# Newton roots on VectorE, a router in four column parts, a hand-ordered token choice and tile-wise memory waits in a two-layer transformer kernel

## The chip, the cores and the metric

The kernel runs on one core of one Trainium2 chip. The metric is the device time of one execution in microseconds (us); lower is better. The engines are PE (TensorE: matmuls and transposes; PEld are its weight loads), DVE (VectorE), ACT (ScalarE), POOL (GpSimd) and SP (SyncE, which here issues most DMAs). Each engine works through its own queue in order.

## The reference

Two layers on x of 2 x 2048 tokens of width 512, with a context of 154 rows per batch, all in float32:

```python
x = x + L0_xattn(layernorm(x), ctx)     # 16 heads of 32, softmax
x = x + L0_ffn(layernorm(x))            # 8 experts; each takes its 1024 best tokens
x = x + L1_xattn(layernorm(x), ctx)     # one head of 512
x = x + L1_ffn(layernorm(x))            # shared part, and 2 of 8 experts per token

def L0_ffn(x):
    scores = softmax(x @ router_w + router_b)
    G, idx = top_k(scores.T, 1024)
    h1 = relu(x[idx] @ w1 + b1)
    eo = h1 @ w2 + b2
    return zeros.at[idx].add(eo * G)

def layernorm(x):
    return (x - mean) / sqrt(var + 1e-5)
```

## The kernel before

The 4096 tokens are 32 tiles of 128 rows (`NT`), in 8 blocks of 4 tiles (`NB`, `TPB`). Five stages follow one another.

**Attention of the first layer.** Inside `tc.manual_schedule` the order on PE, DVE, ACT and POOL is the order in which the program is written. `step(G)` runs for G = 0 to 37; with m, i4 = divmod(G, 4) it handles four heads (i4) of block m, in four quarters. A quarter makes the scores of one token tile (`scores_of`: eight matmuls into the single PSUM tile `sc`, L285, then the row maximum `mx` on DVE, L289, and a subtraction, L290), takes exp on ACT (`exp_of`, L301 and L304) and normalizes the quarter before (`normalize`: sum and reciprocal on DVE, L310 and L311, a product on POOL, L312). Between these stand the transposes `pp` of the previous step's probabilities (L318), the products with the values `av` (L333), the queries of the next block (L186), and behind the attention the output projection (L352), the residual (L357), and the norm and router of older tiles: `norm_x1`, `transpose_x1`, `router`, `logits`, `router_scores`. `router(u)` is called for one tile and multiplies `rw` of 512 x 8; `logits` turns the four results of a block with four small transposes.

`roots(m)` makes the reciprocal standard deviations of one block of x and one of the residual stream: Sqrt on ACT (L161), then a reciprocal on DVE (L162). It is called in the steps with i4 = 2; its readers are `norm_x` and `norm_x1` (L166). After 38 steps a written tail finishes the last block.

**Token choice.** The pools of the attention close. The pool `wm` (weights of the experts, two tags `w1` and `w2` of four buffers of 1 MB) and then `sr` and `pr` open in their memory. Here the order is not written by hand; the framework's scheduler makes it. SP loads the second layer's context weights, then four `w1` and four `w2` tiles. `scores` is turned (L573) and copied to `sco` (L574). A search fixes the 30 bits of each expert's threshold: a count on DVE (L591), a matmul that adds it up per expert (`per_expert`, L579), two small operations on DVE (L594, L595). Then positions are counted, down to `hi` and `lo` (L633, L634). Beside it PE projects the second layer's context (`ps_k`, `ps_kw`, `ps_bqk`, `ps_v`, L643 to L668), whose results go to DRAM (`kw_d`, `vp_d`).

**Experts of the first layer.** The pools `se`, `sm`, `pm` open, again with an order written by hand. `list_head`, `list_part`, `list_sum` and `list_end` make expert 0's token list, `gather` fetches rows of `xs` by index (POOL), `sum_w1` (POOL, L818) and `sum_x` (DVE) prepare sums, and then 16 half-experts run as `hidden` and `outputs`, PE all the time on `product` (L710). POOL adds each result into `xacc` (L901).

**Second layer.** The pools `wh`, `wf`, `sf`, `pf`, `sf1` open. SP loads `kw`, `vp` and the weights of the shared part (L1068 to L1081), then the rows of `xacc` (L1161); steps run over the tiles, and the routed experts follow.

When a pool opens in memory that a closed pool held, its first users wait for everything that used the old pool. Within a pool, a buffer waits for the last use of that buffer alone.

Of the kernel before, what the change touches and what calls it, by code (L numbers as in the profile page):

```python
# [34 lines left out]
E = 8  # L35
# [20 lines left out]
def two_layers(ctx: ExitStack, tc: tile.TileContext, a, out):  # L56
# [36 lines left out]
    def layernorm(src, dst, small):  # L93

        st = small.tile([P, TPB, 6], F32, tag="st", name="st")
        mv = small.tile([P, TPB, 2], F32, tag="mv", name="mv")
        rstd = small.tile([P, TPB], F32, tag="rstd", name="rstd")
        for t in range(TPB):
            nc.vector.bn_stats(st[:, t, :], src[:, t, :])
            nc.vector.bn_aggr(mv[:, t, :], st[:, t, :])  # L100
        nc.scalar.activation(rstd, mv[:, :, 1], AF.Sqrt, bias=eps_t)
        nc.vector.reciprocal(rstd, rstd)
        for t in range(TPB):
            nc.vector.tensor_scalar(
                dst[:, t, :], src[:, t, :], mv[:, t, 0:1], rstd[:, t : t + 1], ALU.subtract, ALU.mult
            )
# [16 lines left out]
    with (  # L123
        tc.tile_pool(name="wa", bufs=1) as wa,
        tc.tile_pool(name="sx", bufs=2) as sx,
# [5 lines left out]
        rw = wa.tile([P, KC, E], F32, name="rw")  # L131
# [26 lines left out]
        def roots(m):  # L158
            mv, rstd = roots_of(m)
            j = slice(0 if 0 <= m - 2 < NB else 1, 2 if m + 3 < NB else 1)  # L160
            nc.scalar.activation(rstd[:, j], mv[:, j, :, 1], AF.Sqrt, bias=eps_t)  # L161
            nc.vector.reciprocal(rstd[:, j], rstd[:, j])  # L162
# [29 lines left out]
        with tc.tile_pool(name="wk", bufs=1) as wkv:  # L192
# [4 lines left out]
            for w, n in ((wk, "w_kT"), (wv, "w_vT"), (wq, "w_qT"), (wo, "w_oT"), (rw, "router_w")):  # L197
                nc.sync.dma_start(w, a[n].rearrange("(k p) n -> p k n", p=P))
# [3 lines left out]
            roots(-3)  # L202
# [12 lines left out]
            roots(-2)  # L215
# [48 lines left out]
            roots(-1)  # L264
# [6 lines left out]
        with tc.tile_pool(name="sa", bufs=2) as sa:  # L271
# [89 lines left out]
            def norm_x1(u, eng=nc.vector):  # L361
                blk, i = divmod(u, TPB)
                row[u] = sa.tile([P, ROW], F32, tag="row", name="row", bufs=8)
                norm(row[u][:, 0:D], x1t.pop(u), blk + 2, 0, i, eng)

            def transpose_x1(u):
                x1T[u] = sa.tile([P, KC, P], F32, tag="x1T", name="x1T", bufs=4)
                transpose_tile(row[u][:, 0:D], x1T[u], 0, pa, "gen", 3)

            def router(u):  # L370
                blk, i = divmod(u, TPB)
                if i == 0:
                    lT[blk] = sa.tile([E, TPB, P], F32, tag="lT", name="lT")
                ps = pa.tile([E, P], F32, tag="gen", name="ps_l", bufs=3)
                for k in range(KC):
                    nc.tensor.matmul(ps, rw[:, k, :], x1T[u][:, k, :], start=k == 0, stop=k == KC - 1)
                nc.scalar.copy(lT[blk][:, i, :], ps)
# [3 lines left out]
            def logits(blk):  # L381
                pl = pa.tile(SL, F32, tag="gen", name="pl", bufs=3)
                for t in range(TPB):
                    nc.tensor.transpose(pl[:, t, :], lT[blk][:, t, :], ident[0:E, 0:E])
                lg = sa.tile(SL, F32, tag="lg", name="lg")
                lm = sa.tile([P, TPB, 1], F32, tag="lm", name="lm")
                nc.vector.tensor_tensor(lg, pl, rb_bc.unsqueeze(1).to_broadcast(SL), ALU.add)
# [17 lines left out]
            LAST = NT - TPB  # L405

            def step(G):
                m, i4 = divmod(G, TPB)
                on, before = tile_of(G), tile_of(G - 1)
                if tile_of(G + 16):  # L410
                    load_x(G + 16)
# [6 lines left out]
                if i4 == 2 and m <= NB + 1:  # L418
                    roots(m)
# [6 lines left out]
                if tile_of(G - 11) and G - 11 < LAST:  # L426
                    transpose_x1(G - 11)
                if tile_of(G + 9):
                    norm_x(G + 9, nc.gpsimd)
                if on:  # L430
                    scores_of(G, 1)
# [9 lines left out]
                av = values(G - 2) if tile_of(G - 2) else None  # L441
                if on:
                    scores_of(G, 2)
# [11 lines left out]
                if tile_of(G - 10) and G - 10 < LAST:  # L455
                    norm_x1(G - 10, nc.gpsimd)
                if tile_of(G - 11) and G - 11 < LAST:
                    router(G - 11)
# [9 lines left out]
                if tile_of(G + 15):  # L468
                    stats(xt[G + 15], (G + 15) // TPB - 3, 1, (G + 15) % TPB)
                if i4 == 3 and tile_of(G - 15):  # L470
# [3 lines left out]
            for G in range(LAST + 10):  # L474
                step(G)
            roots(NB + 1)
            transpose_x1(LAST - 1)
            router(LAST - 1)
            for u in range(LAST, NT):
                norm_x1(u)  # L480
                transpose_x1(u)
            logits(NB - 2)
            router_scores(NB - 2)
            for u in range(LAST, NT):
                router(u)
            logits(NB - 1)
            router_scores(NB - 1)
# [4 lines left out]
    keep = ctx.enter_context(tc.tile_pool(name="keep", bufs=1))  # L492
# [4 lines left out]
    with tc.tile_pool(name="wm", bufs=4) as wm:  # L497
# [9 lines left out]

        with (
            tc.tile_pool(name="sr", bufs=1) as sr,
            tc.tile_pool(name="pr", bufs=1, space=PSUM) as pr,  # L510
        ):

            ctxT = sr.tile([P, KC, B * TKV], F32, name="ctxT")
            nc.sync.dma_start(ctxT, a["ctxT"].rearrange("(k p) n -> p k n", p=P))
            wk = sr.tile([P, KC, D], F32, name="wk1")
            wv = sr.tile([P, KC, D], F32, name="wv1")
            wqT = sr.tile([P, KC, D], F32, name="wqT1")
            for w, n in ((wk, "Wk"), (wqT, "WqT"), (wv, "Wv")):
                nc.sync.dma_start(w, a[n].rearrange("(k p) n -> p k n", p=P))
            bq = sr.tile([P, KC], F32, name="bq")  # L520
            bk = sr.tile([P, KC], F32, name="bk")
            nc.sync.dma_start(bq, a["bq"])
            nc.sync.dma_start(bk, a["bk"])
            bv_bc = sr.tile([P, D], F32, name="bv_bc")
            nc.sync.dma_start(bv_bc, a["bv"].partition_broadcast(P))
            for q in range(4):
                load_w1(0, q)
            for q in range(4):
                load_w2(0, q)

            def iota(dst, pattern, mult):
                i = sr.tile(dst.shape, I32, name="iota_i")
                nc.gpsimd.iota(i, pattern=pattern, base=0, channel_multiplier=mult)
                nc.vector.tensor_copy(dst, i)

            iota(io128, [[1, P]], 0)
            iota(io8, [[1, CAP // P]], 0)
            iota(io_t, [[1, NT]], 0)
            iota(io_p, [[1, 1]], 1)

            same = sr.tile([P, E, NR], F32, name="same")
            tri = sr.tile([P, E, NR], F32, name="tri")
            nc.gpsimd.affine_select(
                same,
                ones.rearrange("p (e r) -> p e r", e=E),
                pattern=[[-NR, E], [0, NR]],
                compare_op=ALU.is_ge,
                fill=0.0,  # L550
                base=0,
                channel_multiplier=1,
            )
            nc.gpsimd.affine_select(
                same,
                same,
                pattern=[[NR, E], [0, NR]],
                compare_op=ALU.is_ge,
                fill=0.0,
                base=NR - 1,  # L560
                channel_multiplier=-1,
            )
            nc.gpsimd.affine_select(
                tri, same, pattern=[[NR, E], [1, NR]], compare_op=ALU.is_gt, fill=0.0, base=0, channel_multiplier=-1
            )
            same = same.rearrange("p e r -> p (e r)")
            tri = tri.rearrange("p e r -> p (e r)")
            half = RUN // P
            sco = sr.tile([P, half, P], F32, name="sco")
# [4 lines left out]
            nc.vector.tensor_copy(sco, pt)  # L574
            sco = sco.rearrange("p h n -> p (h n)")

            def per_expert(v, m, name):
                ps = pr.tile([P, 1], F32, tag="pc", name=name)
                nc.tensor.matmul(ps, m, v, start=True, stop=True)  # L579
                return ps  # L580
# [3 lines left out]
            thr = sr.tile([P, 1], I32, name="thr")  # L584
            nc.vector.memset(thr, 1 << 29)
            off = sr.tile([P, 1], I32, name="off")
            cmp = sr.tile([P, RUN], F32, name="cmp")
            cnt = sr.tile([P, 1], F32, name="cnt")
# [16 lines left out]
            nc.vector.memset(zero, 0.0)  # L605
# [6 lines left out]
            nc.vector.tensor_scalar(sel, sco, thrf, None, ALU.is_gt, ALU.add, accum_out=cnt)  # L612
            nc.vector.tensor_scalar(eq, sco, thrf, None, ALU.is_equal)
            pc = per_expert(cnt, same, "pc")
# [20 lines left out]


            kw = sr.tile([P, KC, B * TKV], F32, name="kw")
            vp = sr.tile([KV2, B, 2, D], F32, name="vp")
            kpT = sr.tile([P, KC, B * TKV], F32, name="kpT")
            for c in range(KC):  # L640
# [1093 lines left out]
```

## Time and profile before

| | us |
|---|---|
| median of 3 runs (3009.71 to 3010.06) | 3009.86 |
| the profiled execution | 2993.73 |
| its span | 2992.0 |
| PE busy in the span | 2773.7 |
| DVE busy | 1571.9 |
| POOL busy | 1200.7 |
| ACT busy | 883.2 |

The span runs from the first instruction to the last one of one profiled execution; a busy time is the time in which the engine executed something. Times inside the profile count from the start of the span. In the lines of the timeline, the first number is the start, the second the time taken, then engine, line, operation, output <- inputs, sizes and count; brackets give the engine's idle time before and what ended it.

| stretch | what runs there |
|---|---|
| 0 to 60 | loads, keys and values, first queries |
| 60 to 577.6 | 32 steps of the attention |
| 577.6 to 628.1 | the tail, to the last router scores |
| 628.1 to 634.5 | to the first count of the search |
| 634.5 to 683.4 | 30 bits of the search |
| 683.4 to 721.8 | positions, list of expert 0, gathers |
| 721.8 to 2307 | experts of the first layer |
| 2307 to 2325.6 | to the first transpose of the second layer |
| 2325.6 to 2992 | second layer |

### The profile page before, as it was taken

The numbers are of one execution on the slowest core, as the hardware profiler recorded it, in microseconds if no ns is written. First come the engines' busy times: TensorE is split into PE (matmuls) and PEld (weight loads), VectorE is DVE, ScalarE is ACT, GpSimd is POOL, SyncE is SP. The second block draws the span as 40 slices with busy tenths as digits, with TensorE's granted clock in tenths as the row PEclk, the third lists the DMA queues.
The fourth block names the chain that finished last, engine by engine and source line by source line (L and its number), as shares of the span: only waits on it lengthen the run. The fifth ranks groups of instructions, "written<-read, shape, count | busy, mean of one in ns | idle before, by whom it ended". The sixth has DMA issues, their size and how long they took to land. (4 is left out here: it accounts for less than half of the span.)

```text
span 2992.0 us, 38786 instructions
## 1 busy us (share of the span) xinstructions
PE 2773.7 (93%) x14262; PEld 2134.2 (71%) x14262; DVE 1571.9 (53%) x2940; ACT 883.2 (30%) x1859; POOL 1200.7 (40%) x983
## 2 busy tenths in 40 slices
PE   6889999867999999999999999999998788799995
PEld 4444554445888888888888888888887555467774
DVE  4677777544554535435554355354533566553355
ACT  2555555411122112211221122112211555432331
POOL 1445544403334333433343343333331465365552
PEclk9899999978999999999999999999999999899998
DMA  4011111161123131221221312212211732143487
GB/s 161 19 36 43 47 64 44 57 220 39 22 78 89 29 93 54 75 82 25 78 85 43 96 40 81 74 29 78 78 15 45 254 75 75 43 99 128 134 314 288
DMA packets 127083, 256.47 MB, mean 86 GB/s; under 512 B 16508, under 2 KB 22668, under 8 KB 126742
## 3 DMA queue, kind: packets, MB, share of 16 engines
q1 hardware_dynamic: 93232, 170.79, 17.1%
q0 software_dynamic: 29056, 74.81, 10.8%
q10 hardware_dynamic: 4608, 8.39, 0.7%
q8 instruction: 115, 1.88, 0.3%
q14 instruction: 72, 0.59, 0.1%
HBM read 176.09 MB, written 77.85 MB: 85 GB/s over the span
## 5 line engine op out<-in xcount | busy, mean ns | idle before, releaser
L933 POOL TENSOR_TENSOR eo<-eo,b_bc 128x512 f32<-128x512 f32 x63 | 110.2, 1749 | 647.0 <-DVE eo L987 647.0
L832 ACT ACTIVATE H<-H,b_sb 128x256 f32<-128x256 f32 (+1 forms) x384 | 198.9, 571 | 562.3 <-DVE H L883 274.2
L710 PE MATMUL prod<-w2q,H 128*128 128x256 f32 x1536 | 346.9, 379 | 0.0
L710 PEld LDWEIGHTS prod<-w2q,H 128*128 128x128 f32 x1536 | 289.6, 190 | 38.0
L312 POOL TENSOR_TENSOR pr<-pr,sm 128x616 f32<-128x616 f32 x128 | 155.2, 1213 | 273.1 <-DVE sm L311 248.1
L710 PE MATMUL prod<-xsum,sw 128*128 128x256 f32 x1024 | 245.4, 380 | 0.4 <-DVE xsum L793 0.4
L710 PE MATMUL prod<-xgT,w1q 128*128 128x256 f32 x1024 | 243.3, 381 | 0.0
L710 PE MATMUL prod<-xgT,sw 128*128 128x256 f32 x1024 | 243.1, 380 | 0.0
L818 POOL TENSOR_TENSOR sw<-w1q 128x512 f32<-128x512 f32 x128 | 180.0, 1406 | 140.2 <-PE prod L710 139.9
L710 PE MATMUL prod<-tw,hs 128*128 128x256 f32 x1024 | 234.5, 380 | 0.0
L710 PEld LDWEIGHTS prod<-xgT,w1q 128*128 128x128 f32 x1024 | 195.6, 191 | 26.7
L710 PEld LDWEIGHTS prod<-tw,hs 128*128 128x128 f32 x1024 | 192.9, 190 | 27.6 <-PE prod L710 2.3
L710 PEld LDWEIGHTS prod<-xsum,sw 128*128 128x128 f32 x1024 | 193.4, 190 | 26.4 <-POOL sw L818 0.8
L710 PEld LDWEIGHTS prod<-xgT,sw 128*128 128x128 f32 x1024 | 193.5, 190 | 25.6
L113 ACT COPY xgT<-pt 128x512 f32<-128x512 f32 x64 | 37.5, 585 | 431.8 <-PE pt L112 431.8
L289 DVE TENSOR_REDUCE mx<-sc 128x4 f32<-128x616 f32 x128 | 101.8, 795 | 103.0 <-PE sc L285 101.0
L1552 PE MATMUL ph<-xgT,wc 128*128 128x128 f32 x1248 | 152.4, 275 | 3.0 <-DVE wc L1542 2.2
L1552 PEld LDWEIGHTS ph<-xgT,wc 128*128 128x128 f32 x1248 | 145.6, 192 | 4.3 <-issue 4.0
L1567 PE MATMUL po<-wall,h1r 128*128 x312 | 146.7, 593 | 0.0
L1575 DVE TENSOR_TENSOR y<-po,wall 128x512 f32<-128x512 f32 x78 | 53.9, 691 | 142.8 <-PE po L1567 137.5
L901 POOL DMA_INDIRECT xacc<-eo,idx x64 | 100.9, 1576 | 66.6 <-ACT eo L896 63.2
L818 POOL TENSOR_TENSOR sw<-w1q,sw 128x512 f32<-128x512 f32 x64 | 83.0, 1296 | 111.0 <-PE prod L710 111.0
(306 smaller groups left out, 5162.5 us busy)
## 6 DMA issues: line engine op xcount, KB each, us to landing
w1q<-in_w SPq DMA_DIRECT2D x32, 1024.0 KB, 5.2
w2q<-in_w SPq DMA_DIRECT2D x32, 1024.0 KB, 8.5
y<-ys SPq DMA_DIRECT2D x40, 256.0 KB, 7.5
xs<-row SPq DMA_DIRECT2D x32, 260.0 KB, 3.0
x_sb<-in_x SPq DMA_DIRECT2D x32, 256.0 KB, 2.8
x<-in_x SPq DMA_DIRECT2D x32, 256.0 KB, 2.6
xacc<-x SPq DMA_DIRECT2D x32, 256.0 KB, 2.4
x<-xacc SPq DMA_DIRECT2D x32, 256.0 KB, 4.3
```

Source lines behind the costliest of these rows:

```text
L113: nc.scalar.copy(dstT[:, :, ts(t, P)], pt)
L289: nc.vector.tensor_reduce(mx, sc[:, :, 0:TKV], AX.X, ALU.min)
L312: nc.gpsimd.tensor_tensor(pr, pr, sm.to_broadcast([P, 4, TKV]), ALU.mult)
L710: nc.tensor.matmul(ps[:, g, :], w, m, start=i == 0, stop=i == len(terms) - 1)
L818: nc.gpsimd.tensor_tensor(o, l, m, ALU.add if i == 0 else ALU.subtract)
L832: nc.scalar.activation(dst, src, AF.Relu, bias=b1_sb[:, e, f : f + 1])
L901: sc_ = nc.gpsimd.indirect_dma_start(out=xacc[:, :], out_offset=bass.IndirectOffsetOnAxis(ap=idx[:, e, col : col + 1], axis=0), in_=eo, in ...
L933: nc.gpsimd.tensor_tensor(eo, eo, b2_bc, ALU.add)
L1552: nc.tensor.matmul(ph[:, c, :], wc[:, k * HE + c * P : k * HE + (c + 1) * P], x_[:, k, :], start=k == 0, stop=k == KC - 1,)
L1567: nc.tensor.matmul(po_[r], h[:, c, :], wflat[:, bass.ds(at + (W2_AT + c * D), D)], start=c == 0, stop=c == HE // P - 1)
L1575: nc.vector.tensor_tensor(y, po_.pop(r), wflat[:, bass.ds(at + B2_AT, D)], ALU.add)
```

## The change

1. **Roots.** In the first layer's attention Sqrt and reciprocal go; `inverse_roots` makes the reciprocal root with integer arithmetic on the bits and three Newton steps on DVE. It is a generator: `step` runs it in four portions, now in the steps with i4 = 1. The second layer keeps its Sqrt.
2. **Router.** `rw` is padded with zeros to 32 columns per part. `router(blk)` runs once per block, four tiles into four groups of 32 output partitions; `logits` needs one transpose. `transpose_x1` moves from the first to the third quarter, `x1T` becomes a tile per block, `row` gets 12 buffers.
3. **Tail.** 33 steps run instead of 38, and the rest is written out in another order.
4. **Token choice.** Constants (iotas, masks, `sco`, `thr`, ...) are made at the program's start. The context weights are loaded on POOL's queue into buffers of tag `w2`; `load_w2(0, q)` follows when they are done with. The stage is ordered by hand: after each `per_expert` matmul, PE gets a part of the context products (`beside`). The sums of the values' bias move from DVE to ACT and POOL.
5. **Memory.** Most pools get `reuse_waits="tile"`: a tile in reused memory waits only for the tiles that lay there. Some pools take memory from the other side (`side="right"`). The tiles of the lists and gathers move from `sm` and `pm` to new pools `sl` and `pl` that open before the token choice. `sum_w1` of the first half-expert is called before `list_head`.

```diff
-    def layernorm(src, dst, small):
...
+    magic = const.tile([P, TPB * E], I32, name="magic")
+    nc.vector.memset(magic, 0x5F3759DF)
+
+    def inverse_roots(r, v, pool, tag):
...
+        nc.vector.tensor_single_scalar(i, v.bitcast(I32), 1, ALU.arith_shift_right)
+        nc.vector.tensor_tensor(r.bitcast(I32), mg, i, ALU.subtract)
+        for _ in range(3):
+            yield
+            nc.vector.tensor_tensor(w, v, r, ALU.mult)
+            nc.vector.scalar_tensor_tensor(w, w, -0.5, r, ALU.mult, ALU.mult)
+            nc.vector.scalar_tensor_tensor(r, w, 1.5, r, ALU.add, ALU.mult)
...
-        rw = wa.tile([P, KC, E], F32, name="rw")
+        rw = wa.tile([P, KC, HD], F32, name="rw")
+        nc.vector.memset(rw, 0.0)
...
         def roots(m):
...
-            nc.scalar.activation(rstd[:, j], mv[:, j, :, 1], AF.Sqrt, bias=eps_t)
-            nc.vector.reciprocal(rstd[:, j], rstd[:, j])
+            var = sx.tile([P, 2, TPB], F32, tag="var", name="var")
+            nc.vector.tensor_scalar_add(var[:, j], mv[:, j, :, 1], EPS)
+            yield from inverse_roots(rstd[:, j], var[:, j], sx, "root%d" % (j.stop - j.start))
...
-            def router(u):
+            def router(blk):
+                ps = pa.tile([P, P], F32, tag="gen", name="ps_l", bufs=3)
+                x_ = x1T.pop(blk)
                 for k in range(KC):
-                    nc.tensor.matmul(ps, rw[:, k, :], x1T[u][:, k, :], start=k == 0, stop=k == KC - 1)
-                nc.scalar.copy(lT[blk][:, i, :], ps)
+                    for t in range(TPB):
+                        nc.tensor.matmul(
+                            ps[t * HD : (t + 1) * HD, :], rw[:, k, :], x_[:, k, ts(t, P)], start=k == 0, stop=k == KC - 1
+                        )
+                lT[blk] = sa.tile([P, P], F32, tag="lT", name="lT")
+                nc.scalar.copy(lT[blk], ps)
...
             def step(G):
...
+                parts = roots(m) if i4 == 1 else iter(())
...
-                if i4 == 2 and m <= NB + 1:
-                    roots(m)
...
-                if tile_of(G - 11) and G - 11 < LAST:
-                    transpose_x1(G - 11)
                 if tile_of(G + 9):
                     norm_x(G + 9, nc.gpsimd)
+                next(parts, None)
                 if on:
                     scores_of(G, 1)
...
+                next(parts, None)
                 if on:
                     scores_of(G, 2)
...
+                if tile_of(G - 11):
+                    transpose_x1(G - 11)
+                if tile_of(G - 10):
                     norm_x1(G - 10, nc.gpsimd)
-                if tile_of(G - 11) and G - 11 < LAST:
-                    router(G - 11)
+                if i4 == 3 and tile_of(G - 15):
+                    router((G - 15) // TPB)
+                next(parts, None)
                 if on:
                     scores_of(G, 3)
...
+                all_of(parts)
                 if i4 == 3 and tile_of(G - 15):
                     logits((G - 15) // TPB)
                     router_scores((G - 15) // TPB)
...
-            for G in range(LAST + 10):
+            for G in range(NT + 1):
                 step(G)
...
+            residual(u6 + 3, pend.pop("o"))
+            nc.scalar.copy(*av)
+            all_of(roots(L6 + 2))
+            transpose_x1(u5 + 2)
+            norm_x1(u5 + 3, nc.gpsimd)
+            norm_x1(u6, nc.gpsimd)
+            norm_x1(u6 + 1, nc.gpsimd)
+            pend["o"] = project(u7)
+            residual(u7, pend.pop("o"))
...
+            router(L6)
+            for u in range(u7, NT):
+                norm_x1(u)
+                transpose_x1(u)
+            for blk in (L5, L6):
+                logits(blk)
+            router(L7)
+            for blk in (L5, L6):
+                router_scores(blk)
+            logits(L7)
+            router_scores(L7)
...
+        def load_ctx(n, cols):
+            t = wm.tile([P, 4, D], F32, tag="w2", name=n + "1")[:, :, 0:cols]
+            nc.gpsimd.dma_start(t, a[n].rearrange("(k p) n -> p k n", p=P))
+            return t
+
+        sl = outer0.enter_context(tc.tile_pool(name="sl", bufs=2, reuse_waits="tile"))
...
+                def sums(w, m, n):
+                    ps = pr.tile([P, D], F32, tag="pre", name="ps_c", bufs=2)
+                    for k in range(KC):
+                        nc.tensor.matmul(ps[: w(k).shape[1], 0:n], w(k), m(k), start=k == 0, stop=k == KC - 1)
+                        if k < KC - 1 and (k % 2 or n == D):
+                            yield ps
+                    yield ps
...
             def per_expert(v, m, name):
                 ps = pr.tile([P, 1], F32, tag="pc", name=name)
                 nc.tensor.matmul(ps, m, v, start=True, stop=True)
+                next(beside, None)
                 return ps
...
+            for _ in beside:
+                pass
+            for q in range(4):
+                load_w2(0, q)
...
+            sum_w1(0, 0, 0)
+            sum_w1(0, 0, 1)
+            sum_w1(0, 1, 0)
             list_head(0)
...
-            sum_w1(0, 0, 0)
-            sum_w1(0, 0, 1)
-            sum_w1(0, 1, 0)
...
-        sf1 = later.enter_context(tc.tile_pool(name="sf1", bufs=2))
+        sf1 = later.enter_context(tc.tile_pool(name="sf1", bufs=2, side="right", reuse_waits="tile"))
```

## The prediction, written before the result was known

> **What bounds the kernel now.** I read the stage table first, then the order of time inside the stages that the change touches. The table's columns are the stretch in us from the span's start, its length, the busy time of PE, PEld, DVE, ACT and POOL, the granted clock, the DMA share and GB/s.
>
> ```profile
> 60.00:558.30 498.30, 445.59 (x2834) 231.03 (x2834) 353.70 (x709) 257.26 (x615) 236.91 (x166) 0.95 0.14 44
> 577.60:628.10 50.50, 43.88 (x230) 24.55 (x231) 15.88 (x53) 17.56 (x35) 12.27 (x6) 0.93 0.26 92
> 634.50:683.40 48.90, 36.15 (x126) 26.15 (x127) 24.25 (x123) 3.78 (x8) 0.90 (x3) 0.67 0.65 238
> 683.40:705.40 22.00, 16.75 (x48) 6.43 (x46) 8.13 (x21) 0.43 (x1) 0.00 (x0) 0.97 0.15 57
> 721.80:2307.00 1585.20, 1584.69 (x7634) 1391.67 (x7632) 763.51 (x1021) 321.77 (x606) 581.49 (x439) 1.00 0.23 59
> ```
>
> Rows in order: attention, its tail, the search for each expert's threshold, what follows it, the first layer's experts. PE is full for the experts' 1585 us, and the diff leaves their instructions alone: only the 722 us before and the gap after them can move. Before them PE is nearly full in the attention and waits in the search and the lists.
>
> **Roots of the attention.** From the timeline of one step:
>
> ```profile
> 345.73 1.28 ACT L161 ACT_TABLE_LOAD   x1
> ...
> 351.23 1.28 ACT L301 ACT_TABLE_LOAD   x1 [0.35 <-DVE pr L290]
> ...
> 353.25 0.55 PE L285 MATMUL sc<-kT,qT 32*128 32x154 f32 x8 [0.75 <-ACT pr L301]
> ```
>
> Sqrt loads a table on ACT, the next exp loads its own again, and PE's scores wait behind it, since `sc` has one buffer. I timed each step from its first row maximum (L289) to that of the next step. The eight steps with i4 = 2 take 16.85, 17.86, 18.55, 19.12, 18.30, 18.30, 17.87, 19.32; the step before each takes 13.73, 17.51, 14.71, 15.57, 15.57, 15.58, 15.15, 14.11. The differences sum to **-24.2**, and that stall goes.
>
> In its place DVE gets 12 small operations per block (add, shift, subtract, three times three) for a reciprocal. Neighbouring small operations (L387 to L389) take 0.19 us and start 0.22 apart: 12 x 0.22 = 2.6 us, in four portions of 0.66. Nine have two SBUF inputs plus the subtract, ten in all, and that matters while POOL runs:
>
> ```profile
> 767.28 1.27 POOL L818 TENSOR_TENSOR sw<-w1q,sw 128x512 f32<-128x512 f32 x1 [1.24 <-PE prod L710]
> 767.54 1.55 DVE L792 TENSOR_TENSOR tw<-w2q 128x512 f32<-128x512 f32 x1
> ...
> 770.34 0.68 DVE L795 TENSOR_TENSOR tw<-w2q,tw 128x512 f32<-128x512 f32 x1
> ```
>
> The DVE operation that normally takes 0.68 took 1.55 and ended after POOL's. In the attention POOL is busy 237 of 498 us, with L312 (1.21) after each reciprocal and L166 (2.07) twice a step. So each portion can stand behind a POOL operation. In the step at 361 to 377 the first portion meets the norm of 365.16 to 367.23 (some 1.2 us left), the next two meet what is left of L312 behind a 0.66 copy (0.5 each), the fourth about 0.9. Queued behind each portion is the next row maximum, so the exp, so PE's next scores. DVE's idle time before those maxima in that step is 0.80, 0.53, 0.00, and 2.55 before the next step's first. Path: (0.66 + 1.2 - 0.8) + (0.66 + 0.5 - 0.53) + (0.66 + 0.5) + 0 = 2.85 per block; steps 0 to 9 have no L166 on `row` and steps from 23 on none on `xn`, so I take 2.0, **+16** for eight blocks. Bounds: all hidden, 0; or nothing hidden and a whole POOL operation per portion, 2.6 + 2.07 + 3 x 1.21 = 8.3, +66. The value lies nearer to the idle rows than to the full collision.
>
> **Router.** Eight matmuls per tile start 0.97 us in a row (370.76 to 371.73); 21 tiles in the loop cost 20.4 of PE. The new router runs once per block, 32 passes into four column parts. `av` does the same with 512 columns: 16 passes in 1.85 against 0.43 each alone, so the parts do overlap; the closest rate for short ones is `sc`, 8 in 0.47, or 0.059 each: 1.9 per block, 9.4 for five. One transpose for four in `logits` saves 0.25 x 5. PE total -12. But PE then waits sooner: the scores at 371.73 left only 0.22 after the exp that frees their buffer, and moving `transpose_x1` into that quarter uses part of the gain. I take a third, **-4**, bounds -12 and 0.
>
> **Start.** Newton in `roots(-1)` stands before the first row maximum (60.01): +2.4. The exp table load at 61.46 (1.28) goes, as no sqrt table was there. **+1**, bounds 0 and +2.4. The iotas, masks and memsets moved here fall before the matmul that waits for weights until 13.44, and POOL is idle until 10.77; without that cover the iotas at 633 to 635 cost 0.6.
>
> **Tail.** From 577.57 the written order gives PE: pp and av 4.4, transposes and project(27) 4.1, av 1.9, then four projects of 3.6, transposes 22 to 25 (4 x 0.53) and one router 1.9. With the two waits kept (POOL's last norm, 0.9 for av's copy) the last project ends near 607.5 instead of 612.65. Then residual and stats 1.6, Newton 2.6, four norms 2.0, last transpose and copy 1.3, router 1.9 (up to 3 at half rate), logits to scores 2.6: about 12.5 to 13, against 15.5 before (612.65 to 628.13). **-7.5**, bounds -3 (the projects wait for residuals anyway) and -10.
>
> **Search: start and pace.**
>
> ```profile
> 632.84 0.42 DVE L574 COPY sco<-pt_s 128x256 f32<-128x256 f32 x1 [4.52 <-DMA xs<-row]
> ...
> 649.72 2.40 PE L643 MATMUL ps_k<-ctxT,wk 128*128 128x308 f32 x4
> ...
> 672.10 1.28 PE L650 MATMUL ps_kw<-kpT,wqT 128*128 128x308 f32 x4
> ```
>
> The search's tile waits for the row stores because its pool's memory was theirs. With `sco` among the constants, 4.5 of that goes, and the casts between 633.2 and 634.5: **-5**, bounds -4 and -6.4. A bit takes 1.55 alone (636.29 to 637.84), 2.48 with four slow context passes behind the count (650.28 to 652.76), 1.35 with four fast ones (672.66 to 674.01). Now 18 bits carry four such passes and 12 carry two 512-wide ones. The passes turned fast at 656.3 after 8 us of work begun at 648.1, so three bits slow: 3 x 2.48 + 27 x 1.35 = 43.9 against 48.9. I give back 1 for data not yet landed: **-4**; bounds -8 (all fast) and, all slow, 18 x 2.48 + 12 x 2.3 = 72.2, +23. The loads move from SP to POOL's queue, behind its norms in the tail and behind whatever last used the four w2 slots; DMA is mostly idle from 612 to 624, while before, 3.7 MB of context shared 390 GB/s with 8 MB of weights until 665. `load_w2` now stands behind the search on SP: 14.7 us to landing under load, and the first use is over 30 us later. If that cover fails, the wait falls on PE directly.
> [...]
>
> **Lists.**
>
> ```profile
> 691.50 0.29 DVE L634 CAST lo<-pos 128x256 bf16<-128x256 int32 x1
> ...
> 705.40 0.43 DVE L729 TENSOR_TENSOR ohhi<-hi,io 128x256 bf16<-128x256 bf16 x1 [4.49 <-DMA vp_d<-vp]
> ```
>
> The list of expert 0 waits 13.6 us for memory of the search pool: the last context sums, then their store. With its own pool and waits by tile it can follow `lo`: **-13.6**, bounds 0 (the wait stays) and -13.9. PE's wait for `sw` at 725.42 (0.75) goes as the sums precede the gathers: **-0.7**. POOL's six sums (7.7 us) stand before the gathers but fit into the 15 us of last counts and list.
>
> **Second layer.** Its loads wait for `eo` at 2306.98 and the first `xacc` loads, at 2317.51, land behind them (5.6 us, against 2.6 for `x` from the input). Earlier loads would give at most 2.8, and 1.9 on a last scatter that took 8.6 against a median 6.7. **-3**, bounds 0 and -5. Other pools with waits by tile: 0, as their steps wait for data.
>
> **Sum.** +1 - 24.2 + 16 - 4 - 7.5 - 5 - 4 - 13.6 - 0.7 - 3 = -45.0. The profiled execution has a span of 2992.0 and took 2993.7; the runs' median is 3009.86, 17.9 above the span, which I carry over: 2992.0 - 45.0 + 17.9 = **2965**. Its own range is 2950 to 2980.
>
> **Rivals.** (1) DVE paces the attention, slower: each Newton portion stands behind a whole POOL operation. Price 66 for 16 and no gain from the router: 2965 + 50 + 4 = **3019**. It decides from 45 us more, 61 over eight blocks, 7.6 per block. For it: POOL's operation starts right after the reciprocal ahead of each portion. Against: 3.9 us of DVE idle per such step. (2) The search pays: half rate throughout, 2965 + 27 = **2992**. For it: rate 0.67 granted now; against: PE would be busy without a gap, and was fast at 656 and 671 under just that load. (3) The waits by tile don't free the memory: 13.6 and 3 stay, **2982**; the pool's own tiles rotate that way today, which speaks against. (4) Newton hides (4 in all) and the router counts in full: 2965 - 12 - 8 = **2945**.
>
> **Chances.** Forecast 0.60, (1) 0.08, (2) 0.12, (3) 0.08, (4) 0.12. The range reaches from a little under (4) to (2): 2938 to 2992. 0.2% is 6 us, about what a measurement of this kernel can tell from no change: faster 0.91 (part of (1) stays below its price), same 0.02, slower 0.07.
>
> **What would show it.** No ACT table load for sqrt before the second layer; steps with i4 = 1 about 2 us longer and those with i4 = 2 about 3 shorter; Newton operations well over 0.2 us where POOL runs; 32 router passes in about 1.9; the first count within 2 us of the last scores; most bits at 1.35; `ohhi` right after `lo`. Bits at 2.4, or a step of 18 us with i4 = 1, would make it wrong.

## The result, and the profile after

| | before | after |
|---|---|---|
| median of 4 runs, us | 3009.78 | 2971.47 |
| lowest and highest | 3000.90, 3010.06 | 2965.58, 2974.45 |
| profiled execution, its span | 2993.73, 2992.0 | 2970.24, 2968.5 |

The ratio is 0.9877 (95% interval 0.9853 to 0.9901): 38 us less. 45 had been forecast; 2971 lies in the range, 6.5 above the forecast.

The two profiled executions differ by 23.5 us only. The second layer, whose instructions stand in the same order on every engine in both kernels, takes 679.5 in the one after and 666.4 in the one before. Absolute times shift between sets of runs (the four sets of the experiments ran on four chips): in the sets where the kernel before took 3007 to 3010 the second layer takes 678 to 682 in all five profiles of changed kernels, in the sets where it took 2987 to 2992 it takes 659 to 665 in the seven of changed kernels, and 671 in one of the kernel before. (The first profile of before, at 2993.73, stands in the record among the runs of the set of e1 to e4, where before took 2992; so the two profiles come from different sets.) No single kernel was profiled in both sorts of set, so this rests on the second layer's instructions being the same in all of them. Therefore stages ahead of the second layer are compared across profiles, and whole times only with the runs of before in the same set.

The table of stages of the kernel after, with the columns that the prediction named (attention to the first maximum of its last step, tail, search, lists, second layer):

```profile
61.60:545.90 484.30, 427.99 (x2788) 220.53 (x2788) 387.18 (x798) 228.58 (x574) 237.50 (x166) 0.95 0.13 44
545.90:607.60 61.70, 50.52 (x340) 26.40 (x340) 33.47 (x108) 18.37 (x43) 16.52 (x10) 0.89 0.21 74
608.70:667.30 58.60, 42.88 (x156) 23.86 (x156) 26.13 (x120) 5.37 (x11) 15.25 (x17) 0.83 0.62 222
667.30:690.80 23.50, 10.73 (x66) 5.54 (x65) 13.08 (x30) 2.92 (x5) 6.95 (x6) 0.71 0.55 184
...
2289.00:2968.50 679.50, 586.98 (x3064) 413.88 (x3064) 350.39 (x897) 259.23 (x546) 341.73 (x323) 0.95 0.49 153
```

The search is the odd row: it takes 58.6 us, 9.7 more than before. More of the context products now run in it, but PE is busy for only 42.9 of the 58.6. Every other stage ahead of the second layer is shorter or level, but for the start, which is 1.6 longer. The stages, each measured from event to event, in us ("step 31" is the last one of 0 to 31; changed kernels are named as in the experiments):

| stage | before | after | w1_slots_first | sqrt_roots | router_old_place | pool_waits | newton_pool |
|---|---|---|---|---|---|---|---|
| to the first row maximum | 60.0 | 61.6 | 61.8 | 59.2 | 62.1 | 60.5 | 61.0 |
| attention, to the first maximum of step 31 | 498.3 | 484.2 | 487.1 | 498.2 | 484.3 | 483.4 | 472.2 |
| tail, to the last scores | 69.6 | 61.7 | 60.9 | 60.0 | 64.1 | 61.7 | 54.7 |
| to the first count | 6.6 | 1.1 | 1.3 | 1.3 | 1.1 | 1.1 | 1.1 |
| search | 48.9 | 58.6 | 44.5 | 58.3 | 60.3 | 67.6 | 44.3 |
| lists, to the first expert product | 38.4 | 23.5 | 24.0 | 23.8 | 23.7 | 27.2 | 23.9 |
| experts | 1585.6 | 1584.5 | 1584.4 | 1584.7 | 1584.9 | 1584.4 | 1584.9 |
| to the second layer's first transpose | 18.2 | 13.7 | 12.1 | 13.7 | 13.8 | 16.4 | 11.9 |

The differences of after and before sum to -36.6, which agrees with the 38 of the runs; the second layer is left out for the reason above.

**The search after.** From the timeline of POOL, PE and VectorE:

```profile
608.27 1.02 POOL L602 DMA_DIRECT2D Wk<-in_Wk  x1 [23.44 <-PE pt_s L667]
...
610.08 0.75 POOL L602 DMA_DIRECT2D ctxT<-in_ctxT  x1
...
623.03 2.39 PE L636 MATMUL ps_c<-ctxT,Wk 128*128 128x308 f32 x4 [13.23 <-DMA ctxT<-in_ctxT]
625.22 0.42 PE L672 MATMUL pc<-cnt,same 128*128 128x1 f32 x2
...
625.68 0.16 DVE L683 TENSOR_SCALAR off<-pc 128x1 int32<-128x1 f32 x1 [14.96 <-PE pc L672]
```

POOL stood idle for 23.44 us and then issued the first context load, after the last scores. The first context product waits 13.23 us for ctxT on PE, the count of the second bit is queued behind it, and VectorE waits 14.96 for that count.

**A step with Newton operations after**, the step from 323.60 to 341.54, the same one in which before took 15.57:

```profile
327.19 2.08 POOL L221 TENSOR_SCALAR xn<-x_sb,mv,rstd 128x512 f32<-128x512 f32 x1
327.40 0.58 DVE L212 TENSOR_SCALAR var<-mv 128x8 f32<-128x8 f32 x1
...
330.70 1.22 POOL L367 TENSOR_TENSOR pr<-pr,sm 128x616 f32<-128x616 f32 x1 [1.43 <-DVE sm L366]
331.02 0.92 DVE L152 TENSOR_TENSOR root_w<-var,rstd 128x8 f32<-128x8 f32 x1
...
338.68 0.13 DVE L152 TENSOR_TENSOR root_w<-var,rstd 128x8 f32<-128x8 f32 x1
...
339.05 1.12 DVE L154 SCALAR_TENSOR_TENSOR rstd<-root_w,rstd 128x8 f32<-128x8 f32 x1
```

The operation of L152 takes 0.13 us where POOL is idle and 0.92 where POOL's normalisation (L367) has begun before it; then it ends with POOL's (331.94 and 331.92). At 339.05 it is the part's third operation that is caught. Next in VectorE's queue comes the row maximum, each time; only behind the last part does VectorE still wait for PE, 1.37 us.

**The lists after:**

```profile
674.70 0.29 DVE L723 CAST lo<-pos 128x256 bf16<-128x256 int32 x1
674.90 0.42 DVE L786 TENSOR_TENSOR ohhi<-hi,io 128x256 bf16<-128x256 bf16 x1
```

ohhi follows lo at once; before, 13.6 us lay between them.

### The profile page after: what moved, and what is told of

Its sections match the earlier page's. It is cut to its first block, busy times and chain, and to the rows that moved or that the text cites. A ratio compares the mean times of both kernels' runs of the same rounds, so it can differ in the third digit from the quotient of the medians.

```text
span 2968.5 us, 38768 instructions
## 1 busy us (share of the span) xinstructions
PE 2749.7 (93%) x14238; PEld 2111.8 (71%) x14238; DVE 1605.5 (54%) x3081; ACT 848.4 (29%) x1806; POOL 1209.6 (41%) x993
## 4 chain that ended last, share of the span: by engine, by line
PE 70%; issue 10%; DVE 8%; POOL 4%; ACT 3%; DMA 2%; another core or an unknown queue 0%; SPq 0%; POOLq 0%; DVEq 0%; ACTq 0%
PE prod L767 50%; PE ps_o L407 4%; PE ps_q L241 3%; POOL ys L1634 2%; PE av L388 2%; PE av L1298 2%; PE pp L373 2%; PE sc L340 2%; DVE mx L344 1%; PE ps_s L1345 1%; PE pt L160 1%; PE ps_c L636 1%; PE sc L1266 1%; PE ps_sr L1320 1%; POOL xg L1582 1%
## 5 line engine op out<-in xcount | busy, mean ns | idle before, releaser
L367 POOL TENSOR_TENSOR pr<-pr,sm 128x616 f32<-128x616 f32 x128 | 155.5, 1215 | 259.3 <-DVE sm L366 230.0
L344 DVE TENSOR_REDUCE mx<-sc 128x4 f32<-128x616 f32 x128 | 101.6, 794 | 78.0 <-PE sc L340 77.6
L340 PEld LDWEIGHTS sc<-kT,qT 32*128 32x128 f32 x1024 | 41.2, 188 | 128.6 <-ACT pr L356 70.8
L356 ACT ACTIVATE pr<-sc,mx 128x154 f32<-128x154 f32 x256 | 86.0, 388 | 157.9 <-DVE pr L345 146.9
```

The source lines that it names most:

```text
L340: nc.tensor.matmul(sc[:, hh, 0:TKV], qT[blk][rr, c, ts(t, P)], kT[rr, b, c, :], start=True, stop=True)
L344: nc.vector.tensor_reduce(mx, sc[:, :, 0:TKV], AX.X, ALU.min)
L356: nc.scalar.activation(pr[:, hh, :], sc[:, hh, 0:TKV], AF.Exp, bias=mx[:, hh : hh + 1], scale=-1.0)
L367: nc.gpsimd.tensor_tensor(pr, pr, sm.to_broadcast([P, 4, TKV]), ALU.mult)
```

## The experiments

Each changes the kernel after unless it says otherwise. Ratios are to the kernel before in the same set of runs, with their 95% intervals.

**e1, before_again: the kernel before, profiled again.** No edit.

> The kernel before, unchanged, profiled a second time. The first profile of it took 2993.73 us where its timed runs took 3001 to 3010, and the changed kernel's second layer (first transpose of it to the end of the span) took 679.5 us against 666.4 there, with the same instructions in the same order on every engine. Theory A, the second layer varies between executions by itself: this profile takes about 3008, its second layer about 680, and everything before it within 2 us of the first profile. Theory B, the new placement of the second layer's memory costs 13 us: the second layer takes 666 +- 2 again, whatever the whole takes.

It took 2998.7 us, its second layer 671.4, all earlier stages within 0.7 of the first profile. Neither theory has its number. Together with the profiles below (see the result) it shows that the second layer moves between sets of runs by some 15 us with identical instructions. What in it moves was not tried: in the profile of after its PE is busy 587.0 us at a granted clock of 0.95, in w1_slots_first 578.2 at 0.96.

**e2, w1_slots_first: w1's buffers first.** The pool gives its slots in order of first use.

```diff
+            for q in range(4):
+                load_w1(0, q)
             wk = load_ctx("Wk", D)
 ...
-            for q in range(4):
-                load_w1(0, q)
```

> The changed kernel with the four quarters of w1 given their buffers ahead of the four context matrices, nothing else. Theory A, the context loads were late because their first buffer lies over memory that the last logits still used: they are issued near 585 instead of 608, the first context product no longer stands 13 us, the search takes 44 to 47 us instead of 58.7, and the kernel takes about 2958 (-13). [...]

0.9821 (0.9804 to 0.9837). From its timeline:

```profile
586.38 1.02 POOL L602 DMA_DIRECT2D Wk<-in_Wk  x1
...
612.12 2.40 PE L636 MATMUL ps_c<-ctxT,Wk 128*128 128x308 f32 x4
```

The loads go out behind POOL's last norm, 22 us earlier, the first product no longer waits, and the search takes 44.5 us instead of 58.6. So the stall was the wait for the buffer's old content, and it cost 14.1 us. Theory A holds. (Over the loop this version takes 487.1 against 484.2, though its instructions there are the same: the loop moves by some us with edits that don't touch it; see e9.) Which of the attention's last tiles lay under the first slot was not separated.

**e3, sqrt_roots: roots by Sqrt again.**

```diff
-            var = sx.tile([P, 2, TPB], F32, tag="var", name="var")
-            nc.vector.tensor_scalar_add(var[:, j], mv[:, j, :, 1], EPS)
-            yield from inverse_roots(rstd[:, j], var[:, j], sx, "root%d" % (j.stop - j.start))
+            nc.scalar.activation(rstd[:, j], mv[:, j, :, 1], AF.Sqrt, bias=eps_t)
+            nc.vector.reciprocal(rstd[:, j], rstd[:, j])
+            yield
 ...
-                parts = roots(m) if i4 == 1 else iter(())
+                parts = iter(())
 ...
+                if i4 == 2 and m <= NB + 1:
+                    all_of(roots(m))
```

> The changed kernel with the roots of the attention again by Sqrt on ScalarE and a reciprocal, at their old place in every fourth step; all else as changed. Theory A, the Newton steps cost about 13 us of the 29 that the step with the root gave up: the third of four steps is longer by 3.0 to 3.6 each, the second of four shorter by 1.6 each, the attention loop takes 484 + 11 to 16, the kernel about 2985. Rival, the Newton steps are hidden and the longer second steps have another cause: the loop takes 484 + 24 to 29, the kernel about 2998. Second rival, the stall went with another part of the change: no difference over 3.

0.9914 (0.9898 to 0.9931); the attention takes 498.2, 14.0 more than after. Summed over the eight steps of each kind: the third steps (i4 = 2) take 146.1 against 117.2 after, +28.9; the second ones (i4 = 1) 121.1 against 135.0, -13.9. Theory A holds. The stall was worth 28.9 and the Newton steps cost 13.9. And 498.2 is what the kernel before takes (498.3): the loop's other edits, router and transposes, sum to nothing.

**e4, router_tiles: the router tile by tile, behind the late transposes.**

```diff
-                if i4 == 3 and tile_of(G - 15):
-                    router((G - 15) // TPB)
+                if tile_of(G - 12):
+                    router_of(G - 12)
```

Here router_of holds the four products of a tile into 8 partitions and their copy to lT, as before the change.

> The changed kernel with the router again tile by tile, four products of 8 columns for each tile one step behind its transpose, all else as changed (the transposes stay at their new place). Theory A, the router was no part of the path in the loop: the attention loop takes 484 +- 3, the tail behind it 2 to 4 longer, the kernel +1 to +6. Rival, as the prediction's low end had it, the router counts in full: the loop is longer by 12 or more.

0.9949 (0.9932 to 0.9965); the loop takes 501.0, 16.8 more. By its numbers the rival had it, but the place in the step is one that neither kernel uses, so e10 was needed.

**e5, after_again: the kernel after, again.** No edit.

> The changed kernel, unchanged, beside the kernel before on a chip where that took 2992 (if it is the same one). Theory A, the second layer's 679.5 us in its first profile belongs to that execution: here it takes 663 to 668 as in the three variants, the attention loop 484 +- 3, the search 58.6, and the kernel about 2953. Rival, the changed kernel itself has a longer second layer, and one of the variants' other edits happened to cure it: 676 or more, kernel 2966 or more.

0.9870 (0.9853 to 0.9887), attention 484.0, search 58.6: every stage ahead of the second layer within 0.5 of the first profile. The second layer took 677.7, as the rival said, but this was a set in which the kernel before took 3007 instead of 2992, so the comparison with e2 to e4 that I had planned fails. Its three companions, of which two have e2's cure, took 680 to 682 as well, and e9 and e10, without that cure, 660 and 662 in a set with before at 2987. The rival falls by these.

**e6, logits_later: the logits one step later,** on e2's kernel.

```diff
-                if i4 == 3 and tile_of(G - 15):
-                    logits((G - 15) // TPB)
-                    router_scores((G - 15) // TPB)
 ...
+                if i4 == 0 and tile_of(G - 16):
+                    logits((G - 16) // TPB)
+                    router_scores((G - 16) // TPB)
                 av = values(G - 2) if tile_of(G - 2) else None
```

> w1_slots_first (2939), with the logits and the token scores of a block moved from the end of every fourth step to the middle of the step behind it, same instructions. Theory A, the router's saving was lost because VectorE waits 1.8 us for the logits' transpose and spends 2.0 us on them just ahead of the next step's first row maximum: the fourth steps take 15.1 to 16 instead of 18.0, the next ones at most 1 longer, the loop 487 - 8 to - 18, the kernel 2921 to 2931. Rival, these steps are long by TensorE's own work in them: the loop within 3 of 487.

The reason for it, in the timeline of after at the end of a router step:

```profile
370.77 0.18 DVE L366 RECIPROCAL sm<-sm 128x4 f32<-128x4 f32 x1
372.79 0.19 DVE L446 TENSOR_TENSOR lg<-pl,rb_bc 128x32 f32<-128x32 f32 x1 [1.84 <-PE pl L443]
...
374.71 0.79 DVE L344 TENSOR_REDUCE mx<-sc 128x4 f32<-128x616 f32 x1
```

VectorE waits for the logits' transpose, which PE reaches only after 3.6 us of projection, and the next step's maximum comes 3.9 us after the reciprocal. 0.9820 (0.9797 to 0.9843). The router steps fell from 18.02 to 16.52, but the steps behind them rose from 14.53 to 16.72: the loop takes 485.7, within the rival's 3 of 487. But the rival's reason, PE's own work in the router steps, doesn't fit their becoming shorter: the cost moved with the logits. What I hadn't expected is the tail, 54.7 instead of 60.9. The two traces show why: in w1_slots_first VectorE makes the sum for the last probabilities behind the logits (565.86), PE waits 4.07 us for the normalisation that follows, and then runs av in 2.93 us; in logits_later the sum stands ahead of the logits (559.92), PE waits 0.61 and runs av in 1.93. In whole times the gain over e2 is not shown: the intervals cover one another's values.

**e7, newton_spread: the Newton parts over two steps,** on e2's kernel: two parts in the second of four steps, two in the third.

```diff
-                parts = roots(m) if i4 == 1 else iter(())
+                if i4 == 1:
+                    pend["r"] = roots(m)
+                parts = pend["r"] if i4 in (1, 2) and "r" in pend else iter(())
 ...
-                next(parts, None)
+                if i4 == 2:
+                    all_of(parts)
```

The next call ahead of scores_of(G, 3) runs for i4 = 1 alone, and the all_of at the end of the step goes.

> w1_slots_first (2939), with the four parts of the Newton steps over two steps (two parts in the second of four, two in the third, done before the normalisation that needs them) instead of all in the second. Theory A, the price of 13 us comes from three full parts in one step whose gaps on VectorE are then used up: the second steps are shorter by 0.8 to 1.6 each and the third ones at most 0.5 longer, the loop 487 - 4 to - 12. Rival, each part costs what it costs wherever it stands (0.9 us behind POOL, then 0.17 for each instruction): the loop within 3 of 487, what the second steps lose the third ones gain.

0.9827 (0.9808 to 0.9847). Against e5 the second steps lose 11.0 (134.9 to 123.9) and the third ones gain 11.9 (117.1 to 129.1); the loop takes 484.6, 2.5 less than e2. The rival holds: the parts cost what they cost where they stand.

**e8, pool_waits: all 18 tile-wise waits taken back** (each `reuse_waits="tile"` removed).

> The changed kernel with all 18 tile-wise waits taken back: a pool's memory is waited for as a whole. Theory A, the start of the search and the loads owe their gain to the tile-wise waits: gap before the search 1.1 -> 5 to 7, lists 23.5 -> 24 to 30, start of the second layer 13.7 -> 17 to 19, the tail 61.7 as it was because its order is written out; kernel +8 to +18. Rival, the written order alone made the gain: no stage longer by over 2.

0.9933 (0.9916 to 0.9949).

```profile
613.72 1.02 POOL L602 DMA_DIRECT2D Wk<-in_Wk  x1 [30.85 <-DMA xs<-row]
...
630.63 2.39 PE L636 MATMUL ps_c<-ctxT,Wk 128*128 128x308 f32 x4 [22.79 <-DMA w1q<-in_w]
```

Now the context loads wait for the row stores to land, and the first product for its data. Against e5 the search takes 67.6, 9 more, the lists 3.8 more, the start of the second layer 2.8 more. The gap before the first count stays at 1.1: that gain, which theory A put down to the waits, belongs to the rest of the change (the prediction's reason, sco among the constants, was not undone alone). And of the 14.9 us won in the lists the tile-wise waits made 3.8; the other 11 are left to the list's own pool and the order, which weren't taken apart.

**e9, transposes_early: the transposes at their old place,** behind the queries of the step.

```diff
                     pend["q"] = queries(m + 1, i4)
+                if tile_of(G - 11):
+                    transpose_x1(G - 11)
 ...
-                if tile_of(G - 11):
-                    transpose_x1(G - 11)
                 if tile_of(G - 10):
```

> The changed kernel with the transposes of the normed rows back at their old place in the step, behind the queries; the router in column parts stays. Read by stage. Theory A, the late place costs what the column parts save (the loop with Sqrt was 498.2 with both against 498.3 with neither): the loop takes 484 - 4 to - 12. Rival, the place makes no difference: 484 +- 2. Second rival, the early place makes TensorE wait for POOL's norms and for x1T's copy: 486 or more.

The loop takes 481.1, 2.9 less than after in e5: outside the 2 of the rival and short of the 4 of theory A. It may be that the late place costs a little, but this is one profile, and edits that leave the loop's instructions alone moved the loop between 483.4 (e8) and 487.1 (e2).

**e10, router_old_place: transposes and a router tile by tile, both at their old places,** Newton kept: e4's router_of, called with G - 11 behind norm_x1, and e9's edit.

> The changed kernel with transposes and a router tile by tile, both at their old places in the loop, Newton steps kept. Read by stage. Theory A, the router's part of the change is worth nothing in the loop and the 16.8 us more of router_tiles came from the place that I gave it: the loop takes 484 +- 3. Rival, with the Newton steps there is room on TensorE that only the column parts make use of: 494 or more, as in router_tiles (501).

The loop takes 484.3: theory A. The router's part of the change, the column parts and the late transposes together, is worth nothing in the loop, and e4's 16.8 belonged to the place. Beside e9 in the same set, the column parts at the early place take 3.1 less (481.1), about what the late place costs; both differences are no larger than the loop's own spread. In the tail it is worth 2.4 (64.1 against 61.7). A block's router there, from its timeline:

```profile
597.90 3.66 PE L432 MATMUL ps_l<-x1T,rw 128*8 128x128 f32 x32
```

and in the timeline of after:

```profile
596.15 1.82 PE L433 MATMUL ps_l<-x1T,rw 128*32 128x128 f32 x32
```

**e11, newton_pool: the nine Newton operations of a block on POOL,** on e6's kernel, for the blocks in the loop. There they are twelve, four for each of the three Newton steps; shift and subtract stay on VectorE.

```diff
+            if eng is nc.gpsimd:
+                eng.tensor_tensor(w, v, r, ALU.mult)
+                eng.tensor_tensor(w, w, r, ALU.mult)
+                eng.tensor_scalar(w, w, -0.5, 1.5, ALU.mult, ALU.add)
+                eng.tensor_tensor(r, w, r, ALU.mult)
+                continue
```

> [...] Theory A, the price of 13 us is VectorE's time and its 0.9 us waits behind POOL: the second steps are shorter by 1 to 2 each, the loop 485.7 - 6 to - 13. Rival, POOL's own queue becomes late (its probabilities stand behind twelve small operations of some 0.3 to 1 us): the loop 485.7 + 0 to + 20.

0.9763 (0.9750 to 0.9776). The loop takes 472.2, 13.5 less than e6; its eight second steps sum to 122.3 instead of 134.7. From the timeline of POOL in one of them:

```profile
322.48 1.22 POOL L374 TENSOR_TENSOR pr<-pr,sm 128x616 f32<-128x616 f32 x1 [1.43 <-DVE sm L373]
323.65 0.20 POOL L153 TENSOR_TENSOR root_w<-var,rstd 128x8 f32<-128x8 f32 x1
...
325.21 1.21 POOL L374 TENSOR_TENSOR pr<-pr,sm 128x616 f32<-128x616 f32 x1 [0.50 <-DVE sm L373]
```

A part takes 1.1 us (323.65 to 324.71) in a gap that POOL had anyway, behind its own normalisation instead of in its way. Theory A holds, with half a us more than its range in the loop, and nearly the whole price of 13.9 is gone. How much of it was VectorE's own time and how much its waits behind POOL was not separated.

**e12, all_four: e11 and the early transposes of e9 together.** No other edit.

> newton_pool (0.9763 of the kernel before) with the transposes of the normed rows at their old early place as well: w1's buffers first, logits one step later, Newton operations on POOL, transposes early. Theory A, the edits add: loop 472.2 - 2 to - 4, all else as in newton_pool, ratio 0.975. Rival, with POOL now later with the normed rows the early transposes make TensorE wait: loop 472 or more, ratio 0.977 or more.

0.9772 (0.9758 to 0.9785). The loop takes 470.0, 2.2 less than e11, as theory A said; the ratio is the rival's. The two intervals overlap: by time e11 and e12 can't be told apart. e11 is the version to keep, 70 us (2.4%) below the kernel before, of which the change itself made 39.

## Why the prediction was right, and where it was not

| term of the sum | predicted | measured | from |
|---|---|---|---|
| start | +1 | +1.6 | after against before |
| Sqrt stall gone | -24.2 | -28.9 | e3, third steps |
| Newton on VectorE | +16 | +13.9 | e3, second steps |
| router and transposes in the loop | -4 | 0 | e3 with before, e10 with e5 |
| tail | -7.5 | -7.9 | after against before |
| to the first count | -5 | -5.5 | the same |
| search | -4 | +9.7 | the same |
| lists and sums of w1 | -14.3 | -14.9 | the same |
| experts | 0 | -1.1 | the same |
| start of the second layer | -3 | -4.5 | the same |

The signs are right but for one. The total came nearer than its worst term: the search missed by 13.7, and Sqrt (4.7), Newton (2.1) and smaller ones took some of it back, which is luck. (The stages sum to -36.6; the terms of the table sum to 1 more, which the loop's other steps gave back.) The tail's -7.9 was not taken apart, so its agreement with -7.5 doesn't show that its reasons were right.

**The search** is the step that failed, and in it one term: "I give back 1 for data not yet landed". The prediction named what could be late (POOL's norms ahead, "whatever last used the four w2 slots") and then priced it at 1 us, by the idle DMA from 612 to 624. The loads were issued only at 608.3, with the count of the second bit queued behind the product that needed them: 14.1 us by e2. That DMA is idle is no evidence that a load can go; what it waits for is. Without that wait the search takes 44.5, so the pace worked out (43.9) was right, but by luck, by two errors that cancel. In e2 one bit takes 2.49 and one 1.94 instead of three at 2.48. And VectorE's threshold update takes 0.75, 0.58 and 1.25 us instead of 0.16 beside POOL's sums of w1, 2.1 in all; the longest of them:

```profile
626.01 1.25 POOL L875 TENSOR_TENSOR sw<-w1q 128x512 f32<-128x512 f32 x1
626.03 1.25 DVE L684 SCALAR_TENSOR_TENSOR thr<-off,thr 128x1 int32<-128x1 int32 x1
```

On **slow bits**: in e2 PE's first context products run four in 2.40 us from 612.12, and from 616.55 in 1.28: 4.4 us until the faster pace. Two slowed bits are what e2 shows, where the prediction had taken three from the 8 us of the trace before. In e2 the first product finds its data at 612.12. In after the loads were late because they were issued late (608.27 against 586.38), and from 608.7 to 625.3 the DMA engines were busy for 0.97 of the time.

**Sqrt and Newton** each were mis-sized (by 4.7 and 2.1), both from per-step readings. The stall was taken as the third step less the second one; but the second steps are no baseline, as they are longer than third ones without Sqrt (121.9 before against 117.2 after, for eight). Against those it is 3.6 per block, not 3.0. For Newton the mechanism was as put: parts that meet POOL's operation stand behind it, and the median of the first operation shows it (columns: minimum, median, maximum in ns):

```profile
L152 DVE TENSOR_TENSOR root_w<-var,rstd x24: 129/906/919, 83.6 to 529.2; 128x4 f32<-128x4 f32 x15, 128x8 f32<-128x8 f32 x9
```

1.7 us per block was paid (13.9 / 8) where 2.0 had been taken and 2.85 worked out. That working used the step at 361 to 377, which is a fourth step with the logits at its end and not one that carries Newton parts, and the 2.55 of idle time stands before its own first maximum (361.57), not the next. The second step from 327.70 has nearly the same waits (0.78, 0.53, 0.00, and 2.55 at its end); it went from 15.57 to 17.94, 2.4 more. A step of 18 us with i4 = 1 had been named as a sign of being wrong: two of the eight second steps came to it (18.06 and 17.94), while all eight together paid the 13.9. The sign was set too low for single steps, as was the other one, bits at 2.4: after has two (2.48 and 2.45), and most bits take 1.35.

**Router.** A third of the PE time saved was taken as gain. It is 0 in the loop: in sqrt_roots the router step is 0.7 longer than before (17.31 to 18.02), the second of four 0.4 shorter, in the steps from 15 on. The step ends with a chain through VectorE that the saving on PE doesn't shorten, and e6 shows that moving this chain moves the cost with it. That the late transposes use up the gain, as the prediction feared in part, fits e9 and e10 but is within the loop's spread; which of the two it was stays open. The column parts do overlap better than estimated: 32 passes in 1.08 us at 301.43 in the loop, where 1.9 had been put.

**Rivals.** (1) VectorE pacing the attention needed 7.6 per block; 1.7 was paid. (2) The search did pay, but through a late load and not through half rate throughout: a clock of 0.50 was granted to 625.3, while PE mostly waited, and 0.96 from there on. (3) The tile-wise waits do free memory (e8: 9.0 + 3.8 + 2.8). (4) Newton hidden with the router in full: neither came about.

## What to carry to other kernels

A transfer that is moved ahead starts only when its buffer's old content is dead (here at 608.27, and at 586.38 with another buffer): work out what lay there, and give late-freed memory to the loads that are needed late. Where one engine's long operations hold up another's small ones, try the small ones on the engine of the long ones, so that they follow them instead of standing in the next chain's way; here this took 13.5 us off the loop. And compare stages by events, since stages with the same instructions can differ between sets of runs by more than the edit (the second layer took 659 to 682 us in the changed kernels).

## What the runs showed of the hardware

The direction of the interference was new to me. Tiny VectorE operations with two SBUF inputs grew from 0.13 to 0.92 us beside POOL's normalisation (L367), and ended with it. VectorE's reductions were not held up there: in the kernel after, the row maximum (L344) took 0.80 us at 351.74, beside an L367 from 351.38 to 352.59, and no more than 0.80 anywhere in the loop; the statistics of x (L205) took 0.69 at 326.45, beside the L367 at 326.00, and 0.69 to 0.70 in all 25.

Beside POOL's norm (L221, 2.08 us) VectorE was not held up to the end. There `var`, with one input, takes 0.58 us at 327.40 and again at 393.04 (at 128x4, which takes 0.14 to 0.17 alone), and ends 0.8 us after the norm's start. L149 at 328.22, with two SBUF inputs, takes 0.17 while the norm runs on to 329.27. Why only the first 0.8 us of the norm hold VectorE up was not tried.

The other direction isn't settled. Of 24 POOL operations of each kind in e11 none took more than 0.21 us beside a VectorE that was busy 361 of 472 us; but in e11's steps VectorE's operations between are reductions and operations on PSUM for the most part, so what one with two SBUF inputs costs POOL was not shown.
